# Routing weights of a Mamba and mixture-of-experts layer: transposed in 32x32 blocks on VectorE and stored by four DMAs, roots kept in SBUF

## The chip, the cores and the metric

The kernel runs on one core of a Trainium2 chip. The core has five engines, each with its own in-order queue: TensorE (PE in the profile; its weight loads are listed as PEld), VectorE (DVE), ScalarE (ACT), GpSimd (POOL) and SyncE (SP), which here issues nearly all DMAs. The time is the device time of one execution in microseconds; lower is better. All data are 32-bit floats.

## What is computed

A batch is one of 16 sequences of 256 tokens with 256 features. Every token is normalized once; the normalized tokens feed a selective state-space block (512 channels, 16 states) and a mixture of 32 experts of which 8 are kept for each token. Both results are added to the input.

```python
xn = (x - mean) / sqrt(var + 1e-5)
# state-space branch
hidden, gate = split(xn @ W_in)                      # 512 channels each
hidden = silu(causal_conv4(hidden) + conv_bias)
dt, B, C = split(hidden @ W_x, [128, 144])           # 128, 16 and 16 columns
dts = softplus(dt @ W_dt + b_dt)
state[t] = exp(dts[t] * A) * state[t-1] + dts[t] * B[t] * hidden[t]      # A = -exp(A_log), 16 states
y = (sum_n(state * C) + hidden * D) * silu(gate)
# mixture-of-experts branch
probs = softmax(xn @ router_w.T)                     # 32 experts
rw, sel = top_k(probs, 8); rw = rw / sum(rw)
moe = sum_e w_e * ((silu(xn @ w_gate[e]) * (xn @ w_up[e])) @ w_down[e])  # w_e = rw where e is selected, else 0
return x + y @ W_out + moe
```

The program computes all 32 experts densely: the 32 x 96 expert features form 24 chunks of 128, and the 8 kept routing weights (zero for the others) multiply them.

## The kernel before

One pass handles one batch of 256 tokens, 16 passes in all, and neighbouring passes overlap. The body is not written as a loop in execution order. Each piece of work is a small function (a step), and `Plan` decides the order: a step is added with its engine, an assumed length, a due time, the steps that it needs, and the buffers that it takes and gives back. `Plan.order` walks through assumed time; whenever an engine is free it takes the ready step with the earliest due time whose buffers are open. A step of ACT that needs the function table already loaded has its due time shifted by `STAY`. Due times come from `ORIGIN`, `PERIOD` and `RATE` (start and distance of the batches for the state-space part and for the experts) plus an offset for each kind of step in `DUE`, and further ones in `FIRST` and `LAST` for the first and the last batch. The order that comes out is fixed in the program; on the chip each engine works through its own queue and waits on semaphores.

PSUM is divided into rings of banks. Ring g has two banks, taken in turn by everything that is called with `bank(name, "g")`: the gate products `pg` (12 a batch), the gate branch `pgate` (2), one half of the projection `ph_0`, the parameters `px`, one half of the widened steps `pdt_0`, the routing logits `pl`, and, before the change, the roots `std` (in `root`) and the transposed routing weights `pw` (in `turn_weights`). Ring u has two banks for the up products `pu` (12), the turned tokens `pt`, `ph_1`, `pdt_1` and `po`. `acc` has one bank, `da` three.

The expert chain for a pair of chunks q: PE makes `pg_q` and `pu_q` (4 matmuls each, line 479), ACT applies silu to `pg_q` giving `sg_q` (line 492), POOL multiplies `sg_q` by the replicated routing weights `wr` (`weigh`, line 498), DVE multiplies by `pu_q` giving `h_q` (`combine`, line 502), and PE accumulates `h_q` times the down weights in `acc` (line 514).

The state-space chain runs in units: POOL makes `bu` (`feed`, line 635), ACT makes the decay factors `da` in PSUM (line 649), DVE scans (line 657) and multiplies with C giving `pr` (line 667), and a DMA issued by POOL adds `pr` to `y` (`collect`, line 672). `inputs` (line 614, POOL) makes the scan's inputs from `dts` and `hs` once a batch.

The routing weights: `route` (PE) makes the logits, `largest` (DVE) and `expo` (ACT) the exponentials, `choose` (DVE, lines 418 to 435) keeps the eight largest and divides by their sum; the result `rest` has tokens on partitions (128 partitions, 2 token blocks, 32 experts). The experts need them with experts as rows: `turn_weights` (PE, line 441) transposes the two 128x32 blocks into a bank of ring g, `keep_weights` (ACT, line 446) copies 32x256 to SBUF, `send_weights` (SP, line 451) writes it to DRAM in one DMA, and `spread` (SP, line 465) reads it back, each row broadcast over the partitions of its expert, in 4 parts of 6 DMAs.

The normalization: `stats` (DVE), `root` (ACT, line 354) writes sqrt(var + eps) into a bank of ring g, `invert` (DVE, lines 360 to 366) takes the reciprocal twice, once into SBUF for the scale and once back into the bank, and multiplies the latter with the mean for the bias `nmr`; `norm` (ACT) applies them.

Of the kernel before, what the change touches and what calls it, by code (L numbers as in the profile page):

```python
# [11 lines left out]
F32 = mybir.dt.float32  # L12
AF = mybir.ActivationFunctionType
ALU = mybir.AluOpType
# [5 lines left out]
class Plan:  # L20
# [7 lines left out]
    SWITCH = 1.3  # L28
    HANDOVER = dict(PE=0.27, DVE=0.14, ACT=0.12, POOL=0.1, SP=0.1)
    MARGIN = dict(PE=0.4, DVE=0.1, ACT=0.1, POOL=0.1, SP=0.0)  # L30
    STAY = -20.9

    def __init__(self, rings):
        self.size = rings
# [86 lines left out]
def mamba_moe_kernel(  # L121
# [30 lines left out]
    nc = tc.nc  # L152
    P = 128
    B, L, H = x.shape
# [4 lines left out]
    NE, _, I = w_gate.shape  # L159
    HC = H // P  # L160
    EC = E // P
    SPS = L // P
# [13 lines left out]
    SPP = SLOTS // PARTS  # L176
    FAR = 1e30
    SLOWEST = 1e-26
    ORIGIN = -7.8
    PERIOD = 81.9  # L180
    RATE = 81.8

    DUE = dict(
        load_x=-109.0, stats=-46.0, root=-81.0, invert=-71.5, norm=204.5, turn=-280.0,
        keep_turned=-290.0, route=-112.0, largest=-4.5, expo=-61.5, choose=-635.5,
        turn_weights=-268.5, keep_weights=-50.5, send_weights=-5.0, project=-51.5,
        conv_first=167.0, conv_rest=110.0, activate=-200.0, params=-88.0, keep_params=24.5,
        send_params=-100.5, widen=-244.5, steps=-8.0, skip=138.0, clear=31.5, inputs=-19.5,
        fetch=-92.0, feed=56.5, decay=3.0, scan=197.5, read=-90.6, collect=-19.0, spread=-14.0,
        gates=-38.0, ups=29.0, silu=210.5, weigh=-13.5, combine=-63.0, down=34.5, settle=-9.0,  # L190
        gate=18.5, gate_silu=-228.0, fold=165.5, gated=319.0, project_out=66.5, load_again=17.0,
        finish=148.5,
    )
    EARLY = dict(
        load_x=207.0, load_experts=17.0, stats=27.0, turn=145.0, route=95.0, project=269.0,
    )

    FIRST = dict(
        route=-180.5, largest=-120.0, expo=-135.5, choose=169.0, turn_weights=-236.0,
        keep_weights=-73.0, project=205.5, conv_first=-230.0, conv_rest=-172.0, activate=363.5,  # L200
        params=-238.5, keep_params=-137.0, widen=28.5, steps=524.5, skip=-62.5, clear=-105.0,
        inputs=94.0, fetch=-5.0, feed=-63.0, decay=-130.0, scan=-89.0, read=-203.5, collect=16.5,
        spread=-108.0, gates=-17.0, ups=5.5, silu=-96.0, weigh=214.5, combine=221.0, down=7.0,
    )

    LAST = dict(
        fetch=101.5, feed=20.0, decay=16.5, scan=199.5, read=15.5, collect=-67.5, spread=0.5,
        gates=267.0, ups=-12.5, silu=65.0, weigh=-46.0, combine=-50.5, down=-1.5, settle=-49.0,
        gate=-41.0, gate_silu=-122.5, fold=-311.0, gated=236.5, project_out=-113.0, finish=90.0,
    )  # L210
    LEAD = -15.2
    TOPK = 8
    EPS = 1e-5

# [4 lines left out]
    p1 = ctx.enter_context(tc.tile_pool(name="p1", bufs=1))  # L219
# [17 lines left out]
    live = {}  # L237
# [83 lines left out]
    def bank(nm, kind):  # L321
        return take(ps, kind, [P, 512], nm)
# [27 lines left out]
        live["mv", b] = mv  # L350

    def root(b):
        std = bank(f"std_{b}", "g")[:, : 2 * SPS].rearrange("p (i s o) -> p i s o", i=2, s=SPS)
        nc.scalar.activation(std[:, 0], live["mv", b][:, :, 1:2], AF.Sqrt, bias=eps_sb)
        live["std", b] = std

    def invert(b):
        mv, std = live.pop(("mv", b)), live.pop(("std", b))
        rstd = p1.tile([P, SPS, 1], F32, tag="rstd", name=f"rstd_{b}")
        nc.vector.reciprocal(rstd, std[:, 0])  # L360
        nc.vector.reciprocal(std[:, 1], std[:, 0])

        nmr = p1.tile([P, SPS, 1], F32, tag="nmr", name=f"nmr_{b}")
        nc.vector.scalar_tensor_tensor(
            nmr, mv[:, :, 0:1], -1.0, std[:, 1], op0=ALU.mult, op1=ALU.mult
        )
        live["st", b] = rstd, nmr

# [49 lines left out]
    def choose(b):  # L418
        pls = live.pop(("pl", b))
        pe, kept = pls[:, 1], pls[:, 2]  # L420
        top = p1.tile([P, SPS, TOPK], F32, tag="top", name=f"top_{b}")
        rest = p1.tile([P, SPS, NE], F32, tag="rest", name=f"rest_{b}")
        for s in range(SPS):
            nc.vector.max(top[:, s, :], pe[:, s, :])
        for s in range(SPS):
            nc.vector.match_replace(rest[:, s, :], top[:, s, :], pe[:, s, :], -1.0)

        nc.vector.scalar_tensor_tensor(
            kept, rest, 0.0, pe, op0=ALU.is_lt, op1=ALU.mult
        )  # L430
# [3 lines left out]
        nc.vector.tensor_mul(rest, kept, tot.to_broadcast([P, SPS, NE]))  # L434
        live["rest", b] = rest

    def turn_weights(b):
        rest = live.pop(("rest", b))
        pw = bank(f"pw_{b}", "g")
        for s in range(SPS):  # L440
            nc.tensor.transpose(pw[:NE, ts(s, P)], rest[:, s, :], ident)
        live["pw", b] = pw

    def keep_weights(b):
        wT = p1.tile([NE, L], F32, tag="wT", name=f"wT_{b}")
        nc.scalar.copy(wT, live.pop(("pw", b))[:NE, :L])
        live["wT", b] = wT

    def send_weights(b):
        wd = dram.tile([NE, L], F32, tag="wd", name=f"wd_{b}")  # L450
        nc.sync.dma_start(wd, live.pop(("wT", b)))
        live["wd", b] = wd


# [295 lines left out]
    b = 0  # L750
# [11 lines left out]
    steps_of = dict(  # L762
        load_x=load_x, stats=stats, root=root, invert=invert, norm=norm, turn=turn,
        keep_turned=keep_turned, route=route, largest=largest, expo=expo, choose=choose,
        project=project, conv_first=conv_first, conv_rest=conv_rest, activate=activate,
        params=params, keep_params=keep_params, turn_weights=turn_weights,
        keep_weights=keep_weights, widen=widen, steps=steps, skip=skip, inputs=inputs,
        fetch=fetch, spread=spread, gates=gates, ups=expand, silu=silu, combine=combine,
        weigh=weigh, down=down, settle=settle, gate=gate, gate_silu=gate_silu, gated=gated,
        project_out=project_out, load_again=load_again, finish=finish, store=store, feed=feed,  # L770
        clear=clear, fold=fold, send_params=send_params, send_weights=send_weights, collect=collect, decay=decay, scan=scan, read=read,
# [17 lines left out]
    for b in range(B):  # L789
        t = ORIGIN + PERIOD * b  # L790
# [3 lines left out]
            needs=[("turn", b - 1)] if b else [], lands=11.0 if b else 3.5)  # L794
        add("stats", (b,), "DVE", 0.9, t, b, needs=[("load_x", b)],
            takes=[("mv", ("mv", b)), ("st", ("st", b)), ("std", ("rs", b))], gives=[("st", b)])
        add("root", (b,), "ACT", 0.3, t, b, needs=[("stats", b)], takes=[("g", ("std", b))],
            table="sqrt")
        add("invert", (b,), "DVE", 0.4, t, b, needs=[("root", b)],
            gives=[("std", b), ("mv", b)])  # L800
        add("norm", (b,), "ACT", 1.09, t, b, needs=[("invert", b)], takes=[("xn", ("xn", b))],
            gives=[x, ("rs", b)])
        xT = ("xnT", b)
        add("turn", (b,), "PE", 1.0, t, b, needs=[("norm", b)], gives=[("xn", b)],
            takes=[("u", ("pt", b)), ("xnT", xT)])
# [160 lines left out]
```

## Time and profile before

| what | value |
|---|---|
| median of 3 runs | 1340.56 us (1340.4 to 1342.53) |
| the profiled execution | 1340.57 us, of which the span is 1338.8 us |
| mean granted TensorE clock | 0.995 |
| PE, DVE, ACT, POOL busy | 97%, 87%, 84%, 89% of the span |
| PE L479 `pu` and `pg`, L514 `acc` | 368.0, 349.0 and 363.9 us busy, 1536 records each |
| POOL L635 `feed`, 256 times | 702.2 us busy, 2837 ns each |
| DVE L657 scan, 512 times | 608.7 us busy, 1218 ns each |
| PE L441 `pw` | 6.1 us busy, 32 records |
| ACT L354 `root` | 4.2 us busy, 16 times |
| DMA of `wd<-wT` | 16 issues of 32 KB, 5.1 us (median) to landing |

A record of PE is one pass of a matmul; a matmul of 32-bit floats leaves two. The records overlap, as matmuls are pipelined, so the mean duration of a record (380 ns) is longer than the distance from one start to the next, and the timeline is the place to read what an instruction costs PE. The table of waits lists for each pair of instruction and releaser how long the engine stood idle just before the instruction.

### The profile page before, as it was taken

What the parts mean: (1) busy time and instruction counts of PE and PEld (TensorE: products, weight loads), DVE (VectorE), ACT (ScalarE), POOL (GpSimd) and SP (SyncE); (2) the same over time, 40 slices, a digit from 0 to 9 for tenths busy, and PEclk for the clock granted to TensorE, in tenths of its full rate; (3) what the DMA queues carried; (4) which work ended last, traced back from release to release, by engine and by line L of the source; (5) the groups of instructions that cost most, each with busy time, mean ns of one, the idle gap of its engine ahead of it and who ended that gap; (6) DMA issues with size and microseconds to landing.
All of it is one profiled execution on the core that took longest, in us unless ns stands there. A gap on an engine that the chain in (4) does not pass through costs nothing. (4 is left out here: it accounts for less than half of the span.)

```text
span 1338.8 us, 18904 instructions
## 1 busy us (share of the span) xinstructions
PE 1298.2 (97%) x6000; PEld 1110.9 (83%) x6000; DVE 1169.7 (87%) x1735; ACT 1128.9 (84%) x1908; POOL 1187.2 (89%) x835
## 2 busy tenths in 40 slices
PE   8999999999999999999999999999999989999998
PEld 6878888887888878888788888888887878888786
DVE  3789989989899988989789898998998989899887
ACT  5989897988989798887888978899797996979874
POOL 1779999998999989898888999989999899998986
PEclk9999999999999999999999999999999999999999
DMA  9999999997989889898899988988899898998994
GB/s 267 276 224 220 202 221 213 217 222 167 232 205 226 190 193 223 203 205 186 197 209 209 213 182 204 220 200 204 182 227 211 189 206 183 224 203 204 218 210 96
DMA packets 165588, 277.18 MB, mean 207 GB/s; under 512 B 32976, under 2 KB 99568, under 8 KB 165488
## 3 DMA queue, kind: packets, MB, share of 16 engines
q0 software_dynamic: 36576, 133.19, 52.5%
q1 hardware_dynamic: 126272, 142.74, 37.3%
q8 instruction: 47, 0.77, 0.2%
q10 hardware_dynamic: 2640, 0.05, 0.1%
q14 instruction: 53, 0.43, 0.1%
HBM read 137.51 MB, written 5.24 MB: 107 GB/s over the span
## 5 line engine op out<-in xcount | busy, mean ns | idle before, releaser
L635 POOL TENSOR_TENSOR bu<-rep,hs 128x1024 f32<-128x1024 f32 x256 | 702.2, 2837 | 90.8 <-DVE da L657 56.1
L657 DVE TENSOR_TENSOR_SCAN da<-da,bu 128x512 f32<-128x512 f32 x512 | 608.7, 1218 | 40.4 <-ACT da L649 32.2
L649 ACT ACTIVATE da<-dts,a_sb 128x256 f32<-128x256 f32 x1024 | 468.6, 473 | 148.3 <-DVE pr L667 129.5
L479 PE MATMUL pu<-xnT,wu_sb 128*128 128x256 f32 x1536 | 368.0, 384 | 17.2 <-DVE h L502 15.3
L514 PE MATMUL acc<-wd_sb,h 128*128 128x256 f32 x1536 | 363.9, 380 | 0.7 <-DVE h L502 0.7
L479 PE MATMUL pg<-xnT,wg_sb 128*128 128x256 f32 x1536 | 349.0, 380 | 11.6 <-DVE hs L546 6.4
L479 PEld LDWEIGHTS pu<-xnT,wu_sb 128*128 128x128 f32 x1536 | 294.0, 193 | 63.0 <-DVE h L502 20.2
L667 DVE TENSOR_TENSOR pr<-da,rep 128x512 f32<-128x512 f32 x512 | 336.3, 678 | 3.8 <-issue 1.3
L479 PEld LDWEIGHTS pg<-xnT,wg_sb 128*128 128x128 f32 x1536 | 290.2, 190 | 57.6 <-issue 8.6
L514 PEld LDWEIGHTS acc<-wd_sb,h 128*128 128x128 f32 x1536 | 289.9, 191 | 39.5 <-DVE h L502 1.1
L672 POOL DMA_DIRECT2D y<-pr x254 | 308.5, 1253 | 13.6 <-DVE da L657 6.0
L498 POOL TENSOR_TENSOR sg<-sg,wr 128x512 f32<-128x512 f32 x192 | 289.5, 1716 | 27.5 <-DMA wr<-wd 26.1
L502 DVE TENSOR_TENSOR h<-pu,sg 128x512 f32<-128x512 f32 x192 | 131.6, 686 | 83.1 <-POOL sg L498 57.7
L649 ACT ACT_TABLE_LOAD x142 | 182.2, 1283 | 2.5
L492 ACT ACT_TABLE_LOAD x91 | 116.8, 1283 | 1.6
L492 ACT ACTIVATE sg<-pg 128x512 f32<-128x512 f32 x192 | 105.0, 594 | 6.0 <-DVE h L502 3.1
L546 DVE SCALAR_TENSOR_TENSOR hs<-ph,small,hs 128x255 f32<-128x255 f32 (+2 forms) x192 | 90.6, 477 | 6.7 <-ACT hs L537 2.1
L691 POOL TENSOR_TENSOR y<-y 128x512 f32<-128x512 f32 x32 | 67.1, 2189 | 0.0
L525 PE MATMUL ph<-xnT,win_sb 128*128 128x256 f32 x256 | 63.5, 394 | 0.0
L726 PE MATMUL po<-wout_sb,y 128*128 128x256 f32 x256 | 60.8, 380 | 1.5 <-PE acc L514 0.7
L561 PE MATMUL px<-hs,wx_sb 128*32 128x256 f32 (+1 forms) x256 | 61.4, 387 | 0.0
L700 PE MATMUL pgate<-xnT,win_sb 128*128 128x256 f32 x256 | 57.9, 379 | 0.0
(67 smaller groups left out, 783.4 us busy)
## 6 DMA issues: line engine op xcount, KB each, us to landing
y<-pr POOLq DMA_DIRECT2D x254, 512.0 KB, 7.3
rep<-bcd SPq DMA_DIRECT2D x128, 512.0 KB, 6.7
wr<-wd SPq DMA_DIRECT2D x128, 192.0 KB, 5.7
wr<-wd SPq DMA_DIRECT2D x128, 128.0 KB, 6.0
wr<-wd SPq DMA_DIRECT2D x128, 64.0 KB, 5.4
xt<-L_attn_input_states_dram SPq DMA_DIRECT2D x16, 256.0 KB, 4.1
o<-L_attn_input_states_dram SPq DMA_DIRECT2D x16, 256.0 KB, 6.7
out_dram<-o SPq DMA_DIRECT2D x16, 256.0 KB, 4.8
```

Of the source, the lines that this page charges most:

```text
L479: nc.tensor.matmul(p[:, j, :], w[:, hc, ts(c, P)], xs[:, hc, :], start=(hc == 0), stop=(hc == HC - 1),)
L492: nc.scalar.activation(sg, live.pop(("g", b, q)), AF.Silu)
L498: nc.gpsimd.tensor_mul(sg, sg, wr[:, r : r + 2, :])
L502: nc.vector.tensor_mul(h, live.pop(("u", b, q)), live.pop(("sg", b, q)))
L514: nc.tensor.matmul(acc[:, s, :], h[:, j, ts(s, P)], wd_sb[:, c, :], start=(c == 0 and s == 0), stop=(c == FC - 1), skip_group_check=True,)
L546: nc.vector.scalar_tensor_tensor(cv[:, c, k:], ph[:, j, : L - k], cw[:, c, KC - 1 - k : KC - k], cv[:, c, k:], op0=ALU.mult, op1=ALU.add,)
L635: nc.gpsimd.tensor_mul(bu, live["rep", b, g][:, 0:1].to_broadcast([P, CPU, NG, L]), live["hs", b][:, ts(u, CPU), :].unsqueeze(2).to_broadc ...
L649: nc.scalar.activation(da[:, i, :], dts[:, c, :], AF.Exp, scale=a_sb[:, c, n : n + 1])
L657: nc.vector.tensor_tensor_scan(flat, flat, live["bu", k][:, j].rearrange("p n l -> p (n l)"), 0.0, op0=ALU.mult, op1=ALU.add,)
L667: nc.vector.tensor_mul(live["pr", k][:, j], live.pop(("da", m)), live["rep", b, g][:, 1])
L672: nc.gpsimd.dma_start(live["y", b, u].rearrange("p c n l -> p (c n l)"), live.pop(("pr", k)).rearrange("p c n l -> p (c n l)"), accum_op=A ...
L691: nc.gpsimd.tensor_add(y[:, :, 0, :], y[:, :, 0, :], y[:, :, 1, :])
```

## The change

`turn_weights` and `keep_weights` are gone. `choose` now ends with a DVE transpose that turns each 32x32 block of `rest` (128 partitions x 64) by itself into `wT`, a tile of 128 partitions: in each quarter of 32 partitions the experts are on the partitions, and the free axis holds 2 token blocks of 32 tokens. `send_weights` writes the four quarters with four DMAs, each of 64 runs of 32 numbers (128 bytes), where one DMA wrote 32 rows of 256 numbers (1 KB).

`root` writes into the SBUF tile `rstd`; `invert` takes one reciprocal in place, and `nmr` is made from `mv` and `rstd`, both in SBUF.

In the plan, the steps' needs and buffers follow, some lengths change, and `STAY`, `ORIGIN`, `PERIOD`, `RATE`, `LEAD` and almost every entry of `DUE`, `EARLY`, `FIRST` and `LAST` have new values, so that the order of the instructions on each engine is a different one.

```diff
-    STAY = -20.9
+    STAY = -18.3
...
-    ORIGIN = -7.8
-    PERIOD = 81.9
-    RATE = 81.8
+    ORIGIN = -1.8
+    PERIOD = 79.7
+    RATE = 80.2
...
     def root(b):
-        std = bank(f"std_{b}", "g")[:, : 2 * SPS].rearrange("p (i s o) -> p i s o", i=2, s=SPS)
-        nc.scalar.activation(std[:, 0], live["mv", b][:, :, 1:2], AF.Sqrt, bias=eps_sb)
+        std = p1.tile([P, SPS, 1], F32, tag="rstd", name=f"rstd_{b}")
+        nc.scalar.activation(std, live["mv", b][:, :, 1:2], AF.Sqrt, bias=eps_sb)
         live["std", b] = std

     def invert(b):
-        mv, std = live.pop(("mv", b)), live.pop(("std", b))
-        rstd = p1.tile([P, SPS, 1], F32, tag="rstd", name=f"rstd_{b}")
-        nc.vector.reciprocal(rstd, std[:, 0])
-        nc.vector.reciprocal(std[:, 1], std[:, 0])
+        mv, rstd = live.pop(("mv", b)), live.pop(("std", b))
+        nc.vector.reciprocal(rstd, rstd)
         nmr = p1.tile([P, SPS, 1], F32, tag="nmr", name=f"nmr_{b}")
         nc.vector.scalar_tensor_tensor(
-            nmr, mv[:, :, 0:1], -1.0, std[:, 1], op0=ALU.mult, op1=ALU.mult
+            nmr, mv[:, :, 0:1], -1.0, rstd, op0=ALU.mult, op1=ALU.mult
         )
...
         nc.vector.tensor_mul(rest, kept, tot.to_broadcast([P, SPS, NE]))
-        live["rest", b] = rest
-
-    def turn_weights(b):
-        rest = live.pop(("rest", b))
-        pw = bank(f"pw_{b}", "g")
-        for s in range(SPS):
-            nc.tensor.transpose(pw[:NE, ts(s, P)], rest[:, s, :], ident)
-        live["pw", b] = pw
-
-    def keep_weights(b):
-        wT = p1.tile([NE, L], F32, tag="wT", name=f"wT_{b}")
-        nc.scalar.copy(wT, live.pop(("pw", b))[:NE, :L])
+
+        wT = p1.tile([P, SPS, NE], F32, tag="wT", name=f"wT_{b}")
+        nc.vector.transpose(
+            wT.rearrange("p s e -> p (s e)"), rest.rearrange("p s e -> p (s e)")
+        )
         live["wT", b] = wT

     def send_weights(b):
         wd = dram.tile([NE, L], F32, tag="wd", name=f"wd_{b}")
-        nc.sync.dma_start(wd, live.pop(("wT", b)))
+        wT = live.pop(("wT", b))
+        for q in range(P // NE):
+            nc.sync.dma_start(
+                wd.rearrange("e (s q t) -> q e s t", s=SPS, q=P // NE)[q], wT[ts(q, NE)]
+            )
         live["wd", b] = wd
...
-        add("root", (b,), "ACT", 0.3, t, b, needs=[("stats", b)], takes=[("g", ("std", b))],
+        add("root", (b,), "ACT", 0.3, t, b, needs=[("stats", b)],
             table="sqrt")
-        add("invert", (b,), "DVE", 0.4, t, b, needs=[("root", b)],
-            gives=[("std", b), ("mv", b)])
+        add("invert", (b,), "DVE", 0.3, t, b, needs=[("root", b)],
+            gives=[("mv", b)])
...
-        add("choose", (b,), "DVE", 1.2, t, b, needs=[("expo", b)], gives=[("pl", b)])
-        add("turn_weights", (b,), "PE", 0.5, t, b, needs=[("choose", b)],
-            takes=[("g", ("pw", b))], gives=[("rest", b)])
-        add("keep_weights", (b,), "ACT", 0.4, t, b, needs=[("turn_weights", b)],
-            gives=[("pw", b)])
-        add("send_weights", (b,), "SP", 0.5, t, b, needs=[("keep_weights", b)], lands=6.5)
+        add("choose", (b,), "DVE", 1.35, t, b, needs=[("expo", b)], gives=[("pl", b)])
+        add("send_weights", (b,), "SP", 1.8, t, b, needs=[("choose", b)], gives=[("rest", b)], lands=6.5)
```

More of the change, by code (lines that the diff above doesn't have):

```diff
@@ L178, in mamba_moe_kernel @@
     SLOWEST = 1e-26
-    ORIGIN = -7.8
-    PERIOD = 81.9
-    RATE = 81.8
+    ORIGIN = -1.8
+    PERIOD = 79.7
+    RATE = 80.2
     DUE = dict(
[L184 to L192, printed above, removed]
+        load_x=-146.0, stats=-45.5, root=-39.5, invert=-189.5, norm=235.5, turn=-297.0,
+        keep_turned=-116.5, route=-81.5, largest=-193.5, expo=-102.5, choose=-538.5,
+        send_weights=-21.0, project=-77.5, conv_first=328.0, conv_rest=265.5, activate=-374.5,
+        params=-132.0, keep_params=-109.5, send_params=-242.0, widen=-104.5, steps=-17.0,
+        skip=149.0, clear=-5.5, inputs=-96.5, fetch=-122.5, feed=168.5, decay=-16.5, scan=322.5,
+        read=-130.1, collect=-20.0, spread=42.0, gates=-33.5, ups=238.5, silu=300.0, weigh=-19.5,
+        combine=-120.0, down=26.5, settle=-222.0, gate=49.5, gate_silu=-159.0, fold=129.0,
+        gated=378.5, project_out=-121.5, load_again=8.0, finish=-12.5,
@@ L193, in mamba_moe_kernel @@
     )
     EARLY = dict(
-        load_x=207.0, load_experts=17.0, stats=27.0, turn=145.0, route=95.0, project=269.0,
+        load_x=171.0, load_experts=55.0, stats=31.0, turn=155.0, route=63.0, project=243.0,
     )
     FIRST = dict(
-        route=-180.5, largest=-120.0, expo=-135.5, choose=169.0, turn_weights=-236.0,
-        keep_weights=-73.0, project=205.5, conv_first=-230.0, conv_rest=-172.0, activate=363.5,
-        params=-238.5, keep_params=-137.0, widen=28.5, steps=524.5, skip=-62.5, clear=-105.0,
@@ L202, in mamba_moe_kernel @@
-        inputs=94.0, fetch=-5.0, feed=-63.0, decay=-130.0, scan=-89.0, read=-203.5, collect=16.5,
-        spread=-108.0, gates=-17.0, ups=5.5, silu=-96.0, weigh=214.5, combine=221.0, down=7.0,
+        route=-144.0, largest=-26.0, expo=57.5, choose=266.0, project=309.5, conv_first=-246.5,
+        conv_rest=-160.5, activate=289.0, params=-357.5, keep_params=261.5, widen=-38.5,
+        steps=574.5, skip=-263.0, clear=-16.0, inputs=125.0, fetch=4.0, feed=-148.5, decay=-125.5,
+        scan=-243.0, read=-43.0, collect=-97.5, spread=-33.5, gates=-12.5, ups=-178.5, silu=-161.0,
@@ L204, in mamba_moe_kernel @@
+        weigh=288.0, combine=344.0, down=57.0,
     )
     LAST = dict(
-        fetch=101.5, feed=20.0, decay=16.5, scan=199.5, read=15.5, collect=-67.5, spread=0.5,
-        gates=267.0, ups=-12.5, silu=65.0, weigh=-46.0, combine=-50.5, down=-1.5, settle=-49.0,
-        gate=-41.0, gate_silu=-122.5, fold=-311.0, gated=236.5, project_out=-113.0, finish=90.0,
+        fetch=5.5, feed=-85.5, decay=55.5, scan=369.0, read=-177.5, collect=-114.5, spread=-3.5,
+        gates=372.0, ups=44.5, silu=146.0, weigh=51.0, combine=141.5, down=275.5, settle=-6.0,
@@ L210, in mamba_moe_kernel @@
+        gate=-31.5, gate_silu=-75.5, fold=-120.5, gated=412.0, project_out=-172.0, finish=299.5,
     )
-    LEAD = -15.2
+    LEAD = -9.2
     TOPK = 8
@@ L765, in mamba_moe_kernel @@
         project=project, conv_first=conv_first, conv_rest=conv_rest, activate=activate,
-        params=params, keep_params=keep_params, turn_weights=turn_weights,
-        keep_weights=keep_weights, widen=widen, steps=steps, skip=skip, inputs=inputs,
+        params=params, keep_params=keep_params, widen=widen, steps=steps, skip=skip, inputs=inputs,
         fetch=fetch, spread=spread, gates=gates, ups=expand, silu=silu, combine=combine,
```

## Prediction

> **What bounds the kernel now.** I read the engines' shares first, then who waited for whom, then TensorE's (PE's) timeline in a regular stretch, then the rows of the instructions that the change touches. All numbers are of the profiled execution: 1338.8 us of span and 1.77 us around it, 1340.57 us, which is the median of the runs shown (1340.56) to 0.01 us.
>
> ```profile
> PE 1298.2 (97%) x6000; PEld 1110.9 (83%) x6000; DVE 1169.7 (87%) x1735; ACT 1128.9 (84%) x1908; POOL 1187.2 (89%) x835
> ```
>
> PE is busy 97% of the span, with POOL, DVE and ACT all behind it at 84 to 89%. So time is won either where PE has less to do, or where PE waits. Its waits, in the table of waits (total us, times, longest):
>
> ```profile
> PEld pu L479 <- DVE h L502: 20.2, 13, 3.5
> PE pu L479 <- DVE h L502: 15.3, 10, 3.1
> PE pg L479 <- DVE hs L546: 6.4, 11, 1.9
> PE pw L441 <- DVE rest L434: 2.0, 2, 1.3
> ```
>
> Three things hold PE: `pu` waits until VectorE (DVE) has made `h` and so emptied a bank of ring u; `pg` waits until the convolution (`hs`) has emptied a bank of the gate ring g; the routing transpose `pw` waits for the weights. (The PEld row is the weight load of the first wait, not a further loss.) PE's timeline of one regular batch (start us, length us, instruction) shows the price of each:
>
> ```profile
> 533.28 0.38 PE L441 MATMUL pw<-ident,rest 128*32 128x128 f32 x2
> 533.50 1.89 PE L514 MATMUL acc<-wd_sb,h 128*128 128x256 f32 x8
> ...
> 575.91 3.62 PE L479 MATMUL pg<-xnT,wg_sb 128*128 128x256 f32 x16
> 580.98 1.99 PE L479 MATMUL pu<-xnT,wu_sb 128*128 128x256 f32 x8 [1.45 <-DVE h L502]
> ```
>
> From start to start, `pw` takes 533.50 - 533.28 = 0.22 us of PE. A group of 4 matmuls (8 records) takes 1.725 us (531.55 to 533.28 for the group before). The turn at 523.31 and the next at 605.25 are 81.9 us apart. PE's own work in between is 180 matmuls x 0.431 = 77.6, the turn 0.44, the routing 0.81 and `pw` 0.22, together 79.1 us. So a regular batch loses about 2.8 us: 1.62 where `pu` waits for `h` (575.91 + 3.45 = 579.36 to 580.98), 0.58 where `pg` waits for `hs` before 539.26, and small steps between unlike groups.
>
> **PE work and bank waits removed.** `pw` goes: 16 x 0.22 = -3.5 us. Its own waits go: -2.0 us. Ring g has two banks; `root` and `turn_weights` each took one per batch and no longer do. By the instruction order of both programs, `pg_4` reuses the bank of `ph_0` 5.39 us of PE work after `ph_0` ends, and that is where it waits. In the changed order the bank of `ph_0` goes to `pg_7`, 8.62 us behind, and that of the routing logits to `pg_6`, also 8.62 us behind. The waits now are 0.3 to 1.9 us (0.4 in most batches), so 3.2 us more lead should cover them: -6.4 us. Bounds: -3.5 for certain; the two waits 0 to -8.4.
>
> **The reordered queue.** The change also gives new due times to nearly all steps, and every engine's order differs from the start. So I compare the orders where it hurts now. In the stretch above, GpSimd (POOL) does this:
>
> ```profile
> 572.22 2.95 POOL L614 TENSOR_TENSOR hs<-dts,hs 128x1024 f32<-128x1024 f32 x1
> ...
> 576.33 2.65 POOL L635 TENSOR_TENSOR bu<-rep,hs 128x1024 f32<-128x1024 f32 x1
> 578.65 2.78 POOL L498 TENSOR_TENSOR sg<-sg,wr 128x512 f32<-128x512 f32 x2
> ```
>
> The weighing of gates 8 and 9 (578.65) stands behind `inputs` and a feed, although ScalarE (ACT) had their silu done by 574.7. So `h_8` is late and `pu_10` waits. In the changed order the weighing of 8 and 9 stands ahead of the last two feeds and of `inputs`. That should remove this wait. A lengthy wait costs twice, for the granted clock falls afterwards (the row's last columns are PEclk, DMA share, GB/s):
>
> ```profile
> 660.00:670.00 10.00, 7.95 (x29) 6.38 (x28) 5.89 (x9) 6.36 (x10) 10.00 (x9) 0.83 0.81 179
> ```
>
> 0.83 over 10 us is 3.4 us at half clock, 1.7 us lost; `pu` waited 2.05 us just before. It happens four times, three of them after `h` waits: 5.1 us. The page "TensorE: Matmul & The Clock Gate" of the Trainium skill ("Why this matters for your kernels") asks only that idle gaps stay under about 3 us; here gaps of 1.87 and 2.05 us were already followed by half clock, so the measurement decides; by the rule alone these 5.1 us would not belong to the waits and the sum would be 2.6 us higher. The `h` waits with their clock are worth 0 to -(15.3 + 5.1) = -20.4 us; I take half, -10, since the cure is seen in the order but not its timing.
>
> Against it, the new order has leads that the old one hasn't. Its shortest distance from a `pu` group to the `acc` group that needs its `h` was 3.45 us of PE work; now acc of `h_9` comes 1.72 us after `pu_9`, the next turn takes the bank of `pu_6` after 1.72 us, and `pu_8` that of `pu_7` after 2.16 us. `h` itself takes 686 ns. It fits if DVE is free at that moment, and misses by up to 1.2 us if a scan (1218 ns) has just begun. So 0 to 3 x 1.2 = 3.6 us in each of the ten batches (sixth to fifteenth) whose order repeats: 0 to +36 us. I take +5 (0.5 a batch), nearer to nothing, because DVE's order puts each `h` where its `pu` is due, and DVE idles 169 us in all.
>
> **Edits that I cost at nothing.** The rows:
>
> ```profile
> L446 ACT COPY wT<-pw 32x256 f32<-32x256 f32 x16 | 5.7, 354 | 1.0 <-PE pw L441 0.9
> L434 DVE TENSOR_TENSOR rest<-pl,tot 128x64 f32<-128x64 f32 x16 | 3.6, 224 | 0.5
> L361 DVE RECIPROCAL std<-std 128x2 f32<-128x2 f32 x16 | 2.5, 158 | 0.0
> L649 ACT ACT_TABLE_LOAD x142 | 182.2, 1283 | 2.5
> ```
>
> ACT loses the copy (-5.7 us) but the new order has 317 table loads where the old one has 305: +12 x 1.283 = 15.4, net +9.7 us in ACT's 210 us of idle time, 129.5 of it waiting for `pr`. DVE gains a block transpose, which no row shows: nearest is the 128x64 multiply, 224 ns (bounds 158, the smallest op, to 686, the 128x512 one), and loses a reciprocal: 16 x 0.066 = +1.1 us in 169 us idle. SP issues three more DMAs a batch: 3 x 0.31 to 0.59 us (medians of `wd<-wT` and `wr<-wd`), 0.9 to 1.8 us; behind them on SP stand the next `rep` and `wr` loads, whose users are POOL's feed and weighing; PE passes it on only if those run dry, as POOL did for 26.1 us once, in the first batch. If all of it were passed on: ACT +9.7, DVE +1.1 to +8, SP +15 to +28. The pieces that the DMAs write shrink from 1 KB to 128 bytes: 3584 more; the queue q10 spends 0.1% of 16 engines on 2640 packets, 8 ns each, so some 29 us over 16 engines, under 2 us of each.
>
> **Sum.** 1340.6 - 3.5 - 2.0 - 6.4 - 10 + 5 = 1323.7; I forecast 1324.
>
> **Rivals.**
> A, the forecast: 1324, own range 1308 (all `h` waits gone, no new ones: 1340.6 - 11.9 - 20.4) to 1336. Chance 0.52.
> B, the waits only move: PE saves `pw` and its waits, 5.5 us, and what it no longer waits for in ring g it waits for elsewhere: 1335. For it: POOL at 89% and DVE at 87% have little room once PE is quicker. Against: ring g really has two owners fewer. 0.16, a fifth of that within no change.
> C, the shared read. In the changed `invert` the instruction that makes `nmr` reads `mv` and `rstd` both from SBUF; now one of them comes from PSUM, as in every other two-tensor DVE row of the steady part (`pr`, `h`, `o`). If it has to wait out the POOL instruction that is running (a feed occupies POOL 2.32 us, 576.33 to 578.65, and POOL is busy 89%), DVE loses 0.89 x 1.16 = 1.0 us a batch, 16 us, and if PE inherits it all: 1324 + 16 = 1340. Against: DVE's 169 us of idle can take it. 0.10, split over faster 0.02, same 0.05, slower 0.03. The page "SBUF — State Buffer" of the Trainium skill speaks for it: it describes a port pair that GpSimd shares with DVE instructions of two SBUF inputs, taken as an exclusive lock. No row here shows such a wait, as no steady instruction of that form ran.
> D, the other side: DVE, not PE, sets the pace at the three short leads. With the gains at 21.9 (3.5 + 2.0 + 6.4 + 10), the kernel gets slower once each of 30 places misses by over 21.9 / 30 = 0.73 us; with a whole scan each it is 1340.6 - 21.9 + 36 = 1355, midway from the turning point 1348. For it: before, even 6.9 us of lead was not enough for `pu_10`. Against: there it was POOL that was late. 0.17.
> E, no regular wait left: the 16 batches at 78.9 + 0.5 us, and start and end as now (6.5 and 5.7 us, with some 20 us of waits in the first and last batches): 1303. 0.05.
>
> **How the numbers follow.** A measurement of this kernel tells 0.2% (2.7 us) from no change. Faster: 0.52 + 0.13 + 0.02 + 0.05 = 0.72; within: 0.03 + 0.05 = 0.08; slower: 0.03 + 0.17 = 0.20. The range 1306 to 1346 leaves out half of D and E and a little of A.
>
> **What would show it.** Right: no `pg<-hs` row of over 1 us in PE's waits, turns of the regular batches under 81 us apart, PE near 1280 us busy, `nmr` still near 157 ns. B would show new waits of PE with ACT or POOL as releaser; C an `nmr` row of 1 us or more; D PE waiting for `h` at `pt`, `pu_8` and acc of `h_9`. I am wrong if regular batches still take 82 us.

## The result, and the profile after

The changed kernel took 1338.34 us (median of 16 runs, 1331.38 to 1341.36) beside 1340.48 us for the kernel before (16 runs on the same chip, 1338.39 to 1345.93): ratio 0.9976, 95% interval 0.9965 to 0.9987. That is 2.1 us faster by the medians (1.7 to 4.7 us by the interval) where 16.6 were forecast. The profiled execution of the changed kernel took 1333.77 us (span 1332.0, granted clock 0.992), 4.6 us below its median, so it shows the better end of what the kernel does; a second set of runs (`after_again`, below) gave a profile of span 1336.7.

The engines' shares, and TensorE's (PE's) waits (total us, times, longest), of the changed kernel:

```profile
PE 1290.4 (97%) x5968; PEld 1109.9 (83%) x5968; DVE 1174.2 (88%) x1735; ACT 1142.6 (86%) x1904; POOL 1189.2 (89%) x835
```

```profile
PE pu L473 <- DVE h L496: 12.0, 6, 6.9
PE po L720 <- DVE hs L540: 7.8, 9, 1.5
PE pg L473 <- ACT sg L486: 7.0, 3, 3.8
...
PE pg L473 <- DVE hs L540: 2.2, 1, 2.2
```

`pw` is gone (32 records fewer), and the gate products' wait for the convolution fell from 6.4 us in 11 pieces to one of 2.2. But one row is new: `po`, the output projection, waits for the convolution in nine batches. The wait of `pg` for ScalarE's (ACT's) silu grew from 2.4 to 7.0 us. The `h` row fell only from 15.3 to 12.0 us, and now has one piece of 6.9.

Where these waits lie says more than their sums. The two longest rows from the fourth to the sixteenth routing, before (219.87 to 1189.41 us) and then changed (226.59 to 1189.47 us):

```profile
PE pu L479 <- DVE h L502: 12.5, 9, 3.1
PE pg L479 <- DVE hs L546: 6.1, 10, 1.9
```

```profile
PE po L720 <- DVE hs L540: 7.5, 8, 1.5
PE pu L473 <- DVE h L496: 0.6, 1, 0.6
```

In these batches `h` no longer holds PE up; 9.7 of its 12.0 us lie between the second and the third routing. The convolution still holds it up: `po` takes the bank of ring u that `ph_1` had, and waits there where `pg` waited at the bank of `ph_0`.

In the regular stretch the kernel is faster, as the turns in PE's timeline show (662.48 - 581.77 = 80.7 us, 81.9 before):

```profile
581.77 0.60 PE L381 MATMUL pt<-ident,xn 128*128 128x128 f32 x4
...
662.48 0.60 PE L381 MATMUL pt<-ident,xn 128*128 128x128 f32 x4
```

The gain is lost at the start. GpSimd (POOL) in the first batch, then PE, then the stretch of 80 to 90 us (its last columns are granted clock, DMA share, GB/s):

```profile
74.60 4.64 POOL L629 TENSOR_TENSOR bu<-rep,hs 128x1024 f32<-128x1024 f32 x2 [9.46 <-DMA rep<-bcd]
79.19 0.86 POOL L666 DMA_DIRECT2D y<-pr  x1
79.80 1.54 POOL L492 TENSOR_TENSOR sg<-sg,wr 128x512 f32<-128x512 f32 x1
```

```profile
82.13 3.78 PE L473 MATMUL pu<-xnT,wu_sb 128*128 128x256 f32 x8 [6.87 <-DVE h L496]
```

```profile
80.00:90.00 10.00, 7.87 (x23) 6.48 (x24) 8.59 (x14) 7.62 (x13) 8.92 (x7) 0.60 0.93 229
```

POOL stands still for 9.46 us until a replicated B/C block has landed; the weighing of gate 6 (79.80) is behind the two feeds that need it; `h_6`, and with it a bank of ring u, is late, and PE idles 6.87 us; the mean granted clock from 80 to 90 us is 0.60. The kernel before waits for the same transfer, until the same time, without a wait of PE for `h` there, so the late transfer alone does not explain the loss:

```profile
74.44 4.66 POOL L635 TENSOR_TENSOR bu<-rep,hs 128x1024 f32<-128x1024 f32 x2 [5.75 <-DMA rep<-bcd]
```

To see how much is lost where, I worked out TensorE's delay at each routing: the start of `pl` in the timeline less PE's own work in front of it in the program's order (0.431 us a matmul, 0.44 a turn, 0.81 a routing, 0.22 a `pw`, as in the prediction). Half clock counts as lost.

```
delay of PE, us          2nd   3rd   4th   5th   7th  16th routing   4th to 16th
before                   7.0  13.6  14.9  17.2  21.7  54.4           39.5
changed                  5.2  22.2  34.4  35.8  39.0  50.9           16.5
```

From the fourth routing on, the changed kernel loses 23.0 us less. Up to there it loses 19.5 us more. Together with PE's own work (1272.3 us before, 1268.8 after) that is -23.0 + 19.5 - 3.5 = -7.0, which is about the difference of the two profiled spans (1338.8 - 1332.0 = 6.8). In the second profile (span 1336.7, nearer the median) the same working gives some 21 us lost up to the fourth routing and some 19.5 won behind it. Nearly half of the 23.0, 10.9 us, is won at the end: between the fourteenth and the sixteenth routing the kernel before loses 12.2 us, the changed one 1.3.

The rows of the touched instructions, in the table of groups (count, busy us, mean ns of one, idle before):

```profile
L361 DVE SCALAR_TENSOR_TENSOR nmr<-mv,rstd 128x2 f32<-128x2 f32 x16 | 9.4, 587 | 0.6
...
L434 DVE STREAM_TRANSPOSE wT<-rest 128x64 f32<-128x64 f32 x16 | 3.9, 246 | 0.5
```

The block transpose takes 246 ns (the prediction took 224). `nmr` is 160 ns in 13 batches and up to 4.36 us in the other three. Before, it was 156 to 158 ns throughout:

```profile
L364 DVE SCALAR_TENSOR_TENSOR nmr<-mv,std 128x2 f32<-128x2 f32 x16 | 2.5, 157 | 0.6
```

This row turned out to be the key to what the edits cost.

### The profile page after: what moved, and what is told of

Its sections match the earlier page's. It is cut to its first block, busy times and chain, and to the rows that moved or that the text cites. A ratio compares the mean times of both kernels' runs of the same rounds, so it can differ in the third digit from the quotient of the medians.

```text
span 1332.0 us, 18939 instructions
## 1 busy us (share of the span) xinstructions
PE 1290.4 (97%) x5968; PEld 1109.9 (83%) x5968; DVE 1174.2 (88%) x1735; ACT 1142.6 (86%) x1904; POOL 1189.2 (89%) x835
## 4 chain that ended last, share of the span: by engine, by line
PE 44%; DVE 17%; POOL 13%; issue 9%; DMA 8%; ACT 8%; SPq 1%; ACTq 0%; POOLq 0%; DVEq 0%
PE acc L508 11%; PE pg L473 10%; PE pu L473 10%; DVE da L651 6%; DMA rep<-bcd 5%; POOL bu L629 5%; POOL sg L492 5%; PE po L720 4%; PE px L555 4%; DVE hs L540 4%; DVE pr L661 4%; ACT da L643 3%; POOL y L666 2%; DMA y<-pr 2%; PE ph L519 2%
## 5 line engine op out<-in xcount | busy, mean ns | idle before, releaser
L629 POOL TENSOR_TENSOR bu<-rep,hs 128x1024 f32<-128x1024 f32 x256 | 726.7, 2942 | 73.3 <-DVE da L651 34.7
L473 PE MATMUL pu<-xnT,wu_sb 128*128 128x256 f32 x1536 | 360.0, 381 | 12.3 <-DVE h L496 12.0
L666 POOL DMA_DIRECT2D y<-pr x254 | 349.1, 1378 | 14.5 <-DVE h L496 5.2
L473 PEld LDWEIGHTS pg<-xnT,wg_sb 128*128 128x128 f32 x1536 | 294.5, 192 | 51.4 <-ACT sg L486 8.2
L492 POOL TENSOR_TENSOR sg<-sg,wr 128x512 f32<-128x512 f32 x192 | 295.6, 1793 | 32.4 <-ACT rstd L353 24.9
L710 POOL TENSOR_TENSOR y<-y,gs 128x512 f32<-128x512 f32 x30 | 73.8, 2893 | 0.1
L685 POOL TENSOR_TENSOR y<-y 128x512 f32<-128x512 f32 x32 | 71.3, 2230 | 0.0
L720 PEld LDWEIGHTS po<-wout_sb,y 128*128 128x128 f32 x256 | 47.4, 190 | 21.0 <-POOL y L710 7.8
```

What stands on the lines that cost most here:

```text
L473: nc.tensor.matmul(p[:, j, :], w[:, hc, ts(c, P)], xs[:, hc, :], start=(hc == 0), stop=(hc == HC - 1),)
L492: nc.gpsimd.tensor_mul(sg, sg, wr[:, r : r + 2, :])
L629: nc.gpsimd.tensor_mul(bu, live["rep", b, g][:, 0:1].to_broadcast([P, CPU, NG, L]), live["hs", b][:, ts(u, CPU), :].unsqueeze(2).to_broadc ...
L666: nc.gpsimd.dma_start(live["y", b, u].rearrange("p c n l -> p (c n l)"), live.pop(("pr", k)).rearrange("p c n l -> p (c n l)"), accum_op=A ...
L720: nc.tensor.matmul(po[:, s, :], y[:, j, 0, ts(s, P)], wout_sb[:, c, :], start=(c == 0 and s == 0), stop=(c == EC - 1), skip_group_check=True,)
```

## Experiments

"Old order" and "new order" are the sequences of steps that the two plans produce. Where an experiment takes an order as it is, the kernel issues the steps from a list, and a step is put back only while what it needs is not there yet:

```diff
-    plan.issue()
+    was, now = [old order without turn_weights and keep_weights], [new order]
+    start = was[: was.index(CUT)]
+    for st in follow(plan, start + [n for n in now if n not in start]):
+        st["fn"](*st["args"])
```

**Is it the edits or the order?** Four kernels beside the kernel before (1341.72 us). First all edits of the change with the whole old order, which separates the edits from the new due times.

> The edits without the new order: every engine keeps the order of the kernel before, with the two transposes and the copy of the routing weights left out, the block transpose behind choose, four DMAs where one was, and the roots in SBUF. Theory 1 (the regular batches of the changed kernel gain by the new order, its first three batches lose about 20 us by it): the edits alone bring what leaves PE for good, 3.5 us of pw and some of its waits: 1334 to 1338. Theory 2 (PE waits only move, whatever is done, since DVE and POOL have no room): 1339 to 1341. Theory 3 (the gain of the regular batches comes from the freed gate banks): 1315 to 1325.

Measured: 1367.76 us (1364.04 to 1375.14), ratio 1.0193 [1.0163, 1.0223]. The edits alone make the kernel slower by 26 us, which none of the three theories had. Its `nmr` row has 2251 ns each instead of 157, 36.0 us in all, and ACT waits for it:

```profile
ACT xn L400 <- DVE nmr L390: 14.0, 8, 4.1
```

Next the old order up to the fourth batch's routing (`CUT = ("route", 3)`), then the new one; the new order up to there, then the old one; and the changed kernel once more.

> The changed kernel, whose steps up to the routing of the fourth batch are issued in the order of the kernel before (without the steps that are gone), the rest in its own order. At that point the kernel before was 14.9 us behind PE's own work and the changed one 34.4. Theory 1: the 19.5 us are kept to the end, 1316 to 1322. Theory 2: the lost time was slack that some engine needs later, and the kernel ends within 5 us of the changed one, 1333 to 1340.

Measured: 1344.19 us, ratio 1.0006 [0.9991, 1.0021].

> The other way round: the changed kernel's order up to the routing of the fourth batch, then the order of the kernel before, with the edits of the changed kernel throughout. Theory 1: it has the bad start and not the good batches, 19 us above the edits alone, 1353 to 1358. Theory 2: 1338 to 1345.

Measured: 1375.41 us, ratio 1.0253 [1.0225, 1.0282].

> The changed kernel once more on the same chip as the three others, for its time beside theirs and a second profile of its start. All theories: 1334 to 1340; theory 1 expects waits of PE of over 10 us in total between 55 and 210 us, and half clock there, as in the first profile.

Measured: 1337.24 us (1333.28 to 1341.99), ratio 0.996 [0.9944, 0.9976].

Old order in the later batches costs some 38 us beside the changed kernel (1375.41 - 1337.24), far more than the 23 of the delays, and its `nmr` has 1999 ns each. So the shared read may hide inside the comparison of the orders. `old_start` did not come out ahead of the changed kernel, which would have spoken against the start; but its `nmr` row has 895 ns each, and the splice itself is not clean (shown below). Neither verdict can be read before the shared read is taken out.

**The shared read by itself.** One edit to the kernel before: `nmr` takes its second operand from SBUF.

```diff
         nc.vector.scalar_tensor_tensor(
-            nmr, mv[:, :, 0:1], -1.0, std[:, 1], op0=ALU.mult, op1=ALU.mult
+            nmr, mv[:, :, 0:1], -1.0, rstd, op0=ALU.mult, op1=ALU.mult
         )
```

> The kernel before with one operand changed: nmr is made from mv and the reciprocal in SBUF instead of the one in the gate bank. Everything else, the gate bank and the second reciprocal too, stays. Theory 4 (with both inputs in SBUF the instruction waits out what POOL is doing, about 2.1 us a batch on DVE, and the old order passes it on to PE): nmr near 2250 ns as in the edits alone, 1362 to 1372. Rival (the four DMAs or the block transpose made the edits slow): nmr may be longer, the time stays at 1339 to 1345.

Measured: 1361.34 us (1359.73 to 1369.41) beside 1340.91, ratio 1.0173 [1.0146, 1.02]. One operand of 16 instructions costs 20 us. VectorE (DVE) and POOL at one of them:

```profile
374.94 5.07 DVE L364 SCALAR_TENSOR_TENSOR nmr<-mv,rstd 128x2 f32<-128x2 f32 x1
379.93 1.22 DVE L657 TENSOR_TENSOR_SCAN da<-da,bu 128x512 f32<-128x512 f32 x1
```

```profile
375.68 3.08 POOL L635 TENSOR_TENSOR bu<-rep,hs 128x1024 f32<-128x1024 f32 x1
377.99 1.99 POOL L691 TENSOR_TENSOR y<-y 128x512 f32<-128x512 f32 x1
```

`nmr`'s record begins at 374.94, ahead of the first multiply's (spans on POOL are rough), and ends at 380.01, where the second multiply ends at 379.98: it lasts over two of them, though POOL started the second when `nmr` had long been due. The Trainium skill ("SBUF — State Buffer", "Who interferes with whom") describes an exclusive lock on the port pair that DVE and GpSimd share; this trace agrees, with 5.07 us for an operation of 0.16. That such a wait can last over two of GpSimd's instructions is from this trace alone. In the changed kernel the same instruction comes, in eleven of the sixteen batches, where POOL has no multiply running, only a fill:

```profile
572.81 2.95 POOL L629 TENSOR_TENSOR bu<-rep,hs 128x1024 f32<-128x1024 f32 x1
...
575.11 1.58 POOL L603 MEMSET y<- 128x512 f32 x2
...
575.85 0.16 DVE L361 SCALAR_TENSOR_TENSOR nmr<-mv,rstd 128x2 f32<-128x2 f32 x1
```

The remaining comparisons take `nmr` as two instructions that read one tensor each and the other factor through a pointer, 209 ns apiece, never more than 215:

```diff
-        nc.vector.scalar_tensor_tensor(
-            nmr, mv[:, :, 0:1], -1.0, rstd, op0=ALU.mult, op1=ALU.mult
-        )
+        for s in range(SPS):
+            nc.vector.tensor_scalar(
+                nmr[:, s, :], mv[:, s, 0:1], rstd[:, s, :], -1.0, ALU.mult, ALU.mult
+            )
```

The edits in the old order, with it:

> The edits without the new order, but nmr made by two small instructions (one for each token block) that read one SBUF tensor, the root's reciprocal being their per-partition scalar. Theory 4: both near 157 ns, and what is left of the edits is their gain on PE: 1330 to 1337. Rival: the time stays above 1355.

Measured: 1340.95 us (1335.69 to 1346.32), ratio 1.0003 [0.9985, 1.0021]: some 27 us less than with the shared read, but no gain over the kernel before and above the 1330 to 1337 expected. Its waits of PE:

```profile
PE pu L503 <- DVE h L526: 15.4, 11, 2.8
PE pu L503 <- DVE hs L570: 4.3, 10, 0.9
PE pt L411 <- DVE h L526: 3.9, 1, 3.9
PE po L750 <- DVE hs L570: 3.1, 2, 1.6
```

The 6.4 us in which `pg` waited for `hs` are now 4.3 us in which `pu` does, in ten batches. The freed banks moved the wait on by one group.

The changed kernel with it:

> The changed kernel in its own order with the same two small instructions for nmr. In the profile of the changed kernel nmr was slow in three batches of sixteen (9.4 us in all, 2.6 if each took 160 ns). Theory 4: no slow nmr, and 0 to 8 us off the changed kernel: 1330 to 1338. If the start's loss comes from the slow nmr at 94 us: half clock before 210 us shrinks, and the time is 1320 to 1330.

Measured: 1334.31 us (1331.16 to 1335.67), ratio 0.995 [0.9931, 0.9969]: about 3 us seem to be what the shared read still costs the changed kernel (1337.24 on the other chip; the two intervals overlap). The delay at the fourth routing is 32.6 us and from there to the sixteenth 16.8.

> The old order up to the routing of the fourth batch, then the new one, with the two small instructions for nmr. Theory 4 with theory 1: PE is 13 to 16 us behind its own work at the fourth routing as in the kernel before (25.3 with the slow nmr) and keeps the new order's regular batches: 1316 to 1326. Theory 2 (the start's loss is slack that is needed later): 1332 to 1340.

Measured: 1337.32 us, ratio 0.9967 [0.9949, 0.9984]. The delay is 20.1 us at the fourth routing and 38.8 at the fifth: the place where the orders meet costs 18.7 us. At ("route", 3) they differ by 14 steps, which I take for the reason. The time lies in the range of theory 2, but with this seam the experiment decides nothing about the start.

**Is the start's loss kept?** Splices at places where the two orders all but coincide.

> The changed kernel with the bias nmr taken through a pointer (one SBUF tensor per instruction, no shared read), in the old order up to just before the third batch's routing and in the new order from there; at this place the two orders differ by 6 steps only, so no seam should show. Theory (what the new order loses in its first batches is kept to the end): TensorE's delay behind its own work at the third routing was 15.9 us in the old order and 21.4 in the new one, so 5.5 us below the 1334.3 of the new order with the same nmr: 1329, with the loss between the third and the fourth routing (11.2 us) still there. Rival (a later start is made up by the batches behind it, or the loss is not the order's): 1334 or more, with the delay at the sixteenth routing again near 49.

Measured beside 1342.44 us for the kernel before: 1332.41 us (1329.51 to 1337.32), ratio 0.9924 [0.9898, 0.995]. The wait at 82 us is gone, but just behind the splice `pu` waits:

```profile
127.97 3.78 PE L503 MATMUL pu<-xnT,wu_sb 128*128 128x256 f32 x8 [3.68 <-DVE h L526]
```

The delays at the second, third and fourth routing are 5.4, 19.5 and 29.4 us. Where the old order goes on (`splice_6th`, below) they are 7.4, 14.7 and 17.4: of the 24.0 us that this kernel loses there, 14 are behind the splice, in the new order's part. The time is 3 us above the expected 1329, which fits that, and its interval still overlaps that of `after_ptr`.

> As the splice before the third routing, but the old order is kept until the fourth batch's routing is done and the fifth not begun (the orders differ by 12 steps there). Theory: the delay at the fourth routing is near 18.4 us, not 32.6, and grows from there as in the new order (16.8 us to the sixteenth routing): 12 to 14 us below 1334.3, so 1321 (1318 to 1325), and faster than both kernels. Rival: the delay catches up with that of the new order within some batches: 1332 or more.

Measured: 1330.91 us (1329.37 to 1335.44), ratio 0.9921 [0.9893, 0.9948]. The delay is 17.6 us at the fourth routing as expected, but 30.3 at the fifth: the splice costs 12.7 (its `pt` waits 5.1 us once for `xn`). A miss of the expected 1321, and in size the seam explains it.

> As the other splices, but the old order is kept to the sixth batch's experts (the orders differ by 6 steps or fewer there). Theory: the delay at the seventh routing is near 26.7 us (old order), where the new order had 37.0; 10 us below 1334.3, so 1324, between the splice at the fourth batch and the new order. Rival: 1332 or more.

Measured: 1326.78 us (1323.5 to 1330.66), ratio 0.9884 [0.9856, 0.9912], faster than both kernels. The delays: 17.4 at the fourth, 27.5 at the seventh, 41.8 at the sixteenth routing, where the new order from the start had 32.6, 37.0 and 49.4. The 9.5 us of advantage at the seventh routing are 7.6 at the end, and the time is 7.5 us below `after_ptr` (1334.31; some 9 us by the two ratios, as the chips differ). The 15.2 us of advantage at the fourth routing shrink to 9.5 because the old order itself loses 10.1 us from there to the seventh and the new one 4.4. What is still lost at the seventh routing is kept to the end.

**Which of the freed banks does the new order need?** The new order with both edits undone: roots and turned weights in ring g.

```diff
+        std = bank(f"std_{b}", "g")[:, : 2 * SPS].rearrange("p (i s o) -> p i s o", i=2, s=SPS)
...
+        pw = bank(f"pw_{b}", "g")
...
+        wT = p1.tile([NE, L], F32, tag="wT", name=f"wT_{b}")
+        nc.scalar.copy(wT, live.pop(("pw", b))[:NE, :L])
```

> The changed kernel's order on every engine, but the edits undone: the roots back in a bank of ring g (nmr reads one operand from PSUM, 157 ns), the routing weights turned by TensorE into a bank of ring g, copied by ScalarE and written in one DMA; TensorE's transpose stands 7.7 us of its work behind the routing. It is compared with the new order with pointer nmr (1334.3). Theory (the freed banks are what lets the new order run at 80.5 and not 81.9 us a batch): ring g has two owners more, TensorE waits at pg or pw again, 6 to 15 us of such rows, and TensorE's own work is 3.5 us more: 1344 to 1353. Rival (the new order alone makes the gain, the edits only take 3.5 us of TensorE's work away): 1336 to 1339, with no pg or pw row over 2 us in total.

Measured: 1412.51 us (1409.88 to 1413.0), ratio 1.0514 [1.0485, 1.0543], far above both expectations. It is not quite the same order: in the new order `root` stands between the gate products 8 and 9 and their silu, when both banks of ring g are full, so a root that takes a bank can only stand behind that silu, or ahead of these products, which was not tried. ACT's queue of a regular batch:

```
new order:   da_4_3  rstd  da_5_0  da_5_1  xn  da_5_2  da_5_3  sg_8  sg_9  da_6_0  xnT
banks back:  da_4_3  da_5_0  da_5_1  da_5_2  da_5_3  sg_8  sg_9  std  xn  da_6_0  xnT
```

DVE waits for the root, and PE waits for the normalized tokens in nearly every batch:

```profile
DVE rstd L388 <- ACT std L382: 44.1, 14, 6.1
```

```profile
PE pt L412 <- ACT xn L402: 51.3, 17, 4.5
```

With the routing weights' part alone undone, every other instruction in its place:

> The changed order with pointer nmr and the roots in SBUF, but the routing weights turned by TensorE into a bank of ring g, copied by ScalarE and written in one DMA, 7.7 us of TensorE's work behind the routing; every other instruction stands as in the run with pointer nmr (1334.3). Theory (only the root's bank stood in the new order's way; the turn costs its work): 3.5 us of TensorE's work, 0 to 4 us of waits at pw or at the gate products behind it: 1338 to 1342. Rival (the bank of the turned weights is needed too: a gate product waits in each batch until ScalarE has copied the weights out): pg waits of 1 us or more in most batches, 1350 or more. Third: the row by row price is hidden, 1334 to 1337.

Measured beside 1341.32: 1336.31 us (1332.98 to 1341.64), ratio 0.9961 [0.9946, 0.9975], against 0.995 [0.9931, 0.9969] for `after_ptr`. The intervals overlap: taking the transpose from PE is not shown to be worth anything. From the fourth to the sixteenth routing its delay grows by 11.6 us, with VectorE's transpose by 16.8, which is more than the 2.6 us of twelve `pw` that the delay leaves out, so the regular batches lose nothing by it. The profiled execution is the slowest of its eight (1341.64 us), and its start is the worst of all: some 27 us of delay at the third routing, with one DMA for the weights as before, so the four DMAs are not what makes the start late. The only row of waits at `pw` is

```profile
PE pw L468 <- ACT sg L519: 0.9, 1, 0.9
```

So of the two edits it is the root in SBUF that this order rests on: not by a wait that went, but by a place in ACT's queue that a root in a bank can't have. This is the difference of two runs; the root's bank alone was not put back.

**One move in the start.** The weighing of gates 6 and 7 of the first batch ahead of the feeds that wait for `rep`.

```diff
+    for n in [("weigh", 0, 6), ("combine", 0, 6), ("weigh", 0, 7), ("combine", 0, 7), ("feed", 6), ("feed", 7)]:
+        names.remove(n)
+    k = names.index(("silu", 0, 3)) + 1
+    names[k:k] = [("weigh", 0, 6), ("combine", 0, 6), ("weigh", 0, 7), ("combine", 0, 7), ("feed", 6), ("feed", 7)]
```

> The changed kernel with pointer nmr and one move: in the first batch GpSimd weighs gates 6 and 7 ahead of the two feeds of the fourth unit (which wait 9.7 us for rep, landed at 75 us), and VectorE combines them as soon as they are there. Theory (the place in GpSimd's queue makes the wait of 7.7 us at pu and the half clock behind it): that wait goes, TensorE's delay at the third routing falls from 21.4 to 13 to 17 us, time 1327 to 1331. Rival (the late rep holds the start in any case, through ScalarE's queue, where the silu of the next gates stands behind decay factors that wait for pr): the wait moves to pg or pu of the next pairs, delay at the third routing 19 or more, 1332 to 1335.

Measured: 1335.22 us (1332.28 to 1338.12), ratio 0.9954 [0.9936, 0.9972]; delay at the third routing 20.6 us. The theory falls: the wait for `h` goes and another takes its place.

```profile
84.35 5.97 PE L503 MATMUL pu<-xnT,wu_sb 128*128 128x256 f32 x16 [5.18 <-ACT dts L620]
```

`dts` reads a bank of ring u that `pu` is to get, and stands in ACT's queue behind decay factors that wait for `pr` (4.62 us), which waits for the same late `rep`. POOL's queue alone is not the cause: the late transfer reaches PE through ACT's queue as well.

## Why the prediction was wrong

The sign was right and the size was not: 1324 forecast, 1338.34 measured. That rival C's 1340 lies nearest is chance: it reached it by another sum. By its own steps:

- **"The reordered queue" is the step that failed**, where it says "I compare the orders where it hurts now" and looks at one regular stretch. It took -10 for the waits for `h` with their clock and +5 for short leads. There the mechanism was right and the size too small: from the fourth to the sixteenth routing `pu`'s waits for `h` fell from 12.5 to 0.6 us, and the delay shrank by 23.0 us in all (some 19.5 in the second profile), more than the 18.4 of waits and clock that I took off. But a new order is new in the first batches too, which the sum put at nothing without a reason, and there it lost 19.5 us. `splice_6th` shows that such a loss is kept: 7.6 us of advantage in delay were 7.5 us of time.
- **"PE work and bank waits removed"** took -3.5, -2.0 and -6.4. In the old order these 11.9 us bring nothing (ratio 1.0003 [0.9985, 1.0021]); the gate products' wait became one of the up products, as rival B had it. In the new order the -6.4 failed too: the lead of `pg` was enough in the regular batches, but `po` at the bank of `ph_1`, which the sum did not look at, waits 7.8 us for the same convolution. The transpose's part in the new order is not separable from nothing. Ring g was worth having for another reason, the place of `root`, which the sum does not contain.
- **The +5 for three short leads (rival D)**: PE's waits from the fourth to the sixteenth routing show none of them but one of 0.6 us; the term was about 0.
- **Rival C, the shared read**, was given 1.0 us a batch and a chance of 0.10. It is real and twice as dear: 1.9 us more a batch in the old order (2084 ns instead of 157), 20 us of time. "Against: DVE's 169 us of idle can take it" was wrong: in `before_nmr` ACT waits 12.8 us for `nmr`, and PE's waits for `h` at `acc` grew from 0.7 to 6.4 us and for the turned tokens at `pl` from 0.7 to 5.6. The changed kernel seems to pay only some 3 us, for its order has put `nmr` where 13 of 16 do not wait, eleven of them beside a fill of POOL.
- **Edits costed at nothing**: the block transpose at 246 ns and the smaller DMAs left no wait of PE in the table, and with one DMA (`turn_back`) the start is no better. ACT's 317 table loads are as counted; the 7.0 us in which `pg` waits for silu include one of 3.8 us at 195 us, also in the start; what of it the loads cause is not shown.
- **What would show it**: turns under 81 us apart, yes but for one of 81.1; no `pg` wait for `hs` above 1 us, true of the regular batches only; `nmr` near 157 ns in 13 of 16; PE near 1280 us busy, no, 1290.4.

What stays open: which of the new order's steps between the third and the fourth routing lose the 10 to 12 us there (PE waits 2.2 us for `hs` and 3.8 us for silu, and the granted clock is 0.85 from 160 to 170 us and 0.69 from 190 to 200), and whether due times can be found that keep the old start without a splice. `splice_6th` still loses 4.6 us from the seventh to the eighth routing, where the orders meet; the earlier ones lose 12.7 to 18.7 there. Whether entering the new order costs something wherever it is done, or only where many steps differ, is not shown.

## What to carry to other kernels

A change that comes with a new order of all steps is two changes, and they are told apart by running the edits in the old order; here the edits alone cost 26 us, and without their shared read neither cost nor gained any. Price the first batches of a new order for themselves: a delay of the engine that sets the pace, drawn up batch by batch, showed within one table that 23 us were won and 19.5 given back. An operand moved from PSUM to SBUF is not free for a DVE instruction with a second SBUF operand while GpSimd multiplies; a freed buffer may be worth more for where it lets an instruction stand than for the wait seen at it.

## What the runs showed of the hardware

- In `before_nmr` a DVE instruction of 128x2 numbers with two SBUF operands took up to 6.46 us in place of 0.16; one of 5.07 us spanned two consecutive GpSimd multiplies. Beside a GpSimd fill, in the changed kernel, it took 0.16. With one operand in PSUM it stayed at 157 ns, and as two instructions with the factor through a pointer at 209 ns each.
- In the kernel with both edits undone 51.3 us of waits at `pt`, 17 of them of at most 4.5 us, go with a mean granted clock of 0.973, which is 38 us lost over its span of 1408.6 (0.027 x 1408.6). The delay grows by 89.4 us from the fourth to the sixteenth routing: behind waits of this length the loss is well above the idle time itself.
- Length alone does not decide it. The same wait of PE of 1.97 us, of gate products in the last batch for a silu, was followed by a granted clock of 0.83 in one execution of the changed kernel (`after_again`, 1260 to 1270 us) and of 1.00 in the other (1250 to 1270 us); in `edits_alone` one of 3.03 us (before 610.65) left it at 1.00 from 600 to 630 us. So the prediction's "A lengthy wait costs twice" holds for some waits only.
